# A graph-convolution kernel: a later turn for ScalarE's copies, rows fetched for every 48th quad, gates as tanh

## The chip, the cores and the metric

The kernel runs on one core of one Trainium2 chip. The core has five engines, each with a queue of its own that it works off in order: TensorE (PE in the profile, with its weight loads shown apart as PEld), VectorE (DVE), ScalarE (ACT), GpSimd (POOL) and SyncE (SP). SyncE and GpSimd start DMAs, and 16 DMA engines carry them out. The metric is the device time of one execution in microseconds (us); less is better.

## The reference

One equivariant graph convolution on 12,500 nodes and 400,000 edges (sorted by destination), with a residual and a layer norm behind it. Cut to what matters:

```python
h_s = s @ lin1_ws * a * _inv(S_IN)                       # per node, 64 numbers
h_v = jnp.einsum('nci,cd->ndi', v, lin1_wv) * ...        # per node, 32 x 3 numbers
hid = jax.nn.silu(edge_scalars @ fc_w1 * _inv(R))        # per edge
w = hid @ fc_w2 * _inv(FC_HID)                           # per edge, 224 weights
es, ev = h_s[edge_src], h_v[edge_src]                    # gather of 160 numbers per edge
# five products of w, es, ev and edge_attr: mid_s (96), mid_v (128 x 3)
agg_s = jax.ops.segment_sum(mid_s, edge_dst, n)          # sum at each destination
agg_v = jax.ops.segment_sum(mid_v, edge_dst, n)
pre_s = s @ sc_ws * a + agg_s @ lin2_ws * a              # scaled
pre_v = ...                                              # the same for the vectors
scalars = jax.nn.silu(pre_s[:, :64])
gated = jax.nn.sigmoid(pre_s[:, 64:96])[:, :, None] * pre_v
out = _layernorm(x + concat(scalars, gated))
```

All of it is float32. Silu of a number is the number times its sigmoid, so `scalars` is gated too.

## The kernel before

First the node table `h_tab` (12,500 rows of 160 numbers, 640 bytes each) is computed and written to memory; this is over after some 80 us. Then one long unrolled loop runs over 782 steps. A step works on a *quad*, four tiles of 128 edges. Six steps make a chunk, for which one pair of DMAs fetches the edges' 64 inputs (`es`, line 200, two buffers). The order on every engine is written out by hand: each engine does its instructions in the order in which the Python loop (line 869) issues them.

In step n, in the order of issue:

- `fetch(n + 4)` (line 724) loads the chunk that begins four steps later and the indices (SyncE).
- `fetch_rows(n)` (line 735): some quads, listed in `own` (line 461), are not gathered by GpSimd. SyncE fetches their 512 rows one by one, each with a register move and a DMA of 640 bytes (line 485), in 32 jobs of 16 rows; a job begins with a load of 16 addresses into registers (line 480). `OWN` is the distance of two such quads, and a job goes out on every `EVERY`th step. The rows go into one buffer `hq`, so the jobs of the next such quad begin when VectorE is through with the last one: they hang on `at_bytes` being multiplied on VectorE in step m - OWN + 2 (line 741).
- `gather` (line 452): for every other quad GpSimd issues four indirect DMAs, one for each tile (line 456), into `hg`, which has four buffers. So GpSimd can be four quads ahead of VectorE and no more.
- `weights` (line 490): four matmul halves give the 224 weights of each edge, in `pw` in PSUM (two buffers, line 498).
- In steps in which a node tile is finished, `turn(k)` (line 627) turns the sums of 128 nodes with two transposes on TensorE; VectorE scales them into `z` (line 637). The remaining parts, `gates` (Sigmoid on ScalarE), `gated`, `residual`, `moments`, `root` (Sqrt on ScalarE) and `norm`, follow one to a step for four node tiles at a time.
- VectorE: `one_hot` (line 561), which is its first to need the step's `pw`; four products of `pw` and `hg` into `pr` (lines 508 and 516); `select_quad` (line 570) into `sel`; then sums of finished blocks into `acc` (line 609).
- `sum_up` (line 824) of the quad of two steps ago: TensorE multiplies `sel` and `pr` into `pa` (line 577). When a pair of blocks is complete, `close` copies it to `sa` on ScalarE (line 790).
- `hide(n + 2)` (line 748), for every second quad: a matmul into `misc` (line 447) and silu on ScalarE into `hid` (line 449).
- `output` and `turn_blocks`: transposes of `sa` into `misc` (line 586), copies to `tt` on ScalarE (lines 589 and 591), and after 16 blocks the second linear map (line 601) with a copy `os` on ScalarE (line 604).
- `products_due`: the self-connection, 50 matmuls into `misc` (line 770), added by VectorE (line 771).

`misc` is two PSUM tiles used in turn by `hide`, `turned`, `second`, `turn` and the self-connection (class `Banks`, line 424). Before TensorE writes one again, the engine that read it last must be through.

Of the kernel before, what the change touches and what calls it, by code (L numbers as in the profile page):

```python
# [37 lines left out]
NF = 4  # L38
OWN = 68
BATCH = 16  # L40
EVERY = 2

# [15 lines left out]
def gnn_kernel(  # L58
# [127 lines left out]
    def in_pairs(a):  # L186

        return a.rearrange("o (c k h) -> o h c k", k=KB, h=2)

    ess = {}  # L190

    def load_chunk(c, queue=nc.sync):
        if c in ess:
            return
        t0, halves = chunks[c]
        es = ess[c] = loads.tile([2 * S, SIDE * P], F32, name="es")
        for half, n in enumerate(halves):
            to = es[half * S:(half + 1) * S]
            e0 = (t0 + half * halves[0]) * P
            queue.dma_start(to[:, :n * P], es_t[:, e0:e0 + n * P])  # L200

# [156 lines left out]


    load_chunk(0, nc.gpsimd)  # L360
    nc.gpsimd.dma_start(dt, dst)
    iota = consts.tile([P, W], F32, name="iota")
    nc.vector.tensor_copy(iota, iota_i)
# [73 lines left out]

    def hidden(pool, psum, es, halves, t0, n):

        ph = psum.tile([2 * S, Q * P], F32, name="ph", tag="misc")  # L440
        hid = pool.tile([2 * S, Q * P], F32, name="hid")
        ends = [max(0, min(n, m - t0)) for m in halves]
        assert ends[0] >= ends[1]
        for k, c0, c1 in ((2 * S, 0, ends[1]), (S, ends[1], ends[0])):
            if c1 > c0:
                c = slice(c0 * P, c1 * P)
                nc.tensor.matmul(ph[:k, c], w1[:k, :k], es[:k, t0 * P + c0 * P:t0 * P + c1 * P],  # L447
                                 start=True, stop=True)
                nc.scalar.activation(hid[:k, c], ph[:k, c], AF.Silu, scale=1.0 / math.sqrt(64))  # L449
        return hid  # L450
# [39 lines left out]
    def weights(psum, hid, slots):  # L490

        pw = psum.tile([P, Q, 256], F32, name="pw")
        n = len(slots)
        for t in range(0, n, 2):
            half, c = slots[t]
            m = min(2, n - t)
            assert half == 0 and all(slots[t + k] == (k, c) for k in range(m))
            nc.tensor.matmul(pw[:, t:t + m, :NWT], hid[:m * S, c * P:(c + 1) * P], w2[:m * S, :m],  # L498
                             start=True, stop=True)
        return pw  # L500

# [73 lines left out]
    def add_tile(pa, half, sel, t, pr, start, stop):  # L575

        nc.tensor.matmul(pa[half * ROWS:(half + 1) * ROWS, :NPR],  # L577
                         sel[:, t].rearrange("p k w -> p (k w)"), pr, start=start, stop=stop)

    def turned(psum, sa, tt, b, n):  # L580

        pt = psum.tile([P, 512], F32, name="pt", tag="misc")
        k = n * ROWS
        for four in range(4):
# [3 lines left out]

        nc.scalar.copy(tt[:, :6, b:b + n].rearrange("c (f k) b n -> c f k b n", f=2),  # L589
                       by[:, :2, 1:, :n])  # L590
        nc.scalar.copy(tt[:, 6:, b:b + n], by[:, 2:, 0, :n])  # L591

# [19 lines left out]
    def finish(fin, psum, t0, nt, p, most=NF):  # L612


        whole = nt if p == P else nt - 1
        spans = [(0, nt)] if t0 + nt == tiles_of_nodes else [(k, k + 1) for k in range(nt)]
        xt = fin.tile([P, most, D], F32, name="xt", bufs=2)
# [9 lines left out]
        def turn(k):  # L627
            if not held:
                held.extend(fin.tile([P, most, *shape], F32, name=name) for name, shape in (
                    ("z", [2 * V3]), ("sg", [V3]), ("y", [D]), ("st", [6]), ("mv", [2]),  # L630
                    ("rs", [])))
            z = held[0]
            c = (t0 + k) * P
            pp = psum.tile([P, 2, V3], F32, name="pp", tag="misc")
            for m in range(2):
                nc.tensor.transpose(pp[:, m], acc[:, m, c:c + P], ident[:V3, :V3])  # L636
            return lambda: nc.vector.tensor_scalar(
                z[:, k], pp.rearrange("p m c -> p (m c)"), at[:, t0 + k:t0 + k + 1], None,
                op0=OP.mult)

        def gates():
            z, sg = held[:2]
            nc.scalar.activation(sg[:, :nt], z[:, :nt, :V3], AF.Sigmoid)

        def gated():
            z, sg, y = held[:3]
            for k, m in spans:
                nc.vector.tensor_mul(y[:, k:m, :S], z[:, k:m, :S], sg[:, k:m, :S])  # L648
                nc.vector.tensor_mul(  # L649
                    y[:, k:m, S:].rearrange("p t (c i) -> p t i c", i=3),  # L650
                    z[:, k:m, V3:].rearrange("p t (i c) -> p t i c", i=3),
                    sg[:, k:m, None, S:].to_broadcast([P, m - k, 3, V]))

        def residual():
            y = held[2]
            for k, m in spans:
                nc.vector.tensor_add(y[:, k:m], y[:, k:m], xt[:, k:m])  # L657

        def moments():
            _, _, y, st, mv, _ = held  # L660
            for k in range(nt):
                nc.vector.bn_stats(st[:, k], y[:, k])  # L662
            for k in range(nt):
                nc.vector.bn_aggr(mv[:, k], st[:, k])  # L664

        def root():
            mv, rs = held[4:]
            nc.scalar.activation(rs[:, :nt], mv[:, :nt, 1], AF.Sqrt, bias=eps)  # L668

        def norm():  # L670
            _, _, y, _, mv, rs = held
            nc.vector.reciprocal(rs[:, :nt], rs[:, :nt])  # L672
# [5 lines left out]

        return [lambda k=k: turn(k) for k in range(nt)] + [
            gates, gated, residual, moments, root, norm]  # L680


# [6 lines left out]
    with tc.tile_pool(  # L689
# [34 lines left out]
        def fetch(n):  # L724

            if n < len(steps):
                c, i, tiles = steps[n]
                if i == 0:
                    load_chunk(c)
                for t, _, _ in tiles:  # L730
                    ahead(t)
# [3 lines left out]
        def fetch_rows(n):  # L735

            for m in own:
                if n == max(1, m - OWN - 6):
                    at_of[m] = places(mine, m)
                if n == m - OWN + 2:  # L740
                    nc.vector.tensor_scalar_mul(at_of[m], at_of[m], float(row_bytes))
                    hq_of[m], jobs = rows_of(mine, at_of[m])
                    rows_due.extend((m, job) for job in jobs)
            if n % EVERY == 0 and rows_due:
                rows_due.pop(0)[1]()
            assert all(m > n for m, _ in rows_due)

        def hide(n):
# [4 lines left out]
            if i % 2:  # L753
                return
            load_chunk(c)
            hids[c, i // 2] = hidden(edge, misc_ps, ess[c], chunks[c][1], 2 * i, 4)

        CHN = 500

        def self_connection(c0):  # L760
# [13 lines left out]
            return [lambda: part(0, scs, xs), lambda: part(1, scv, xv)]  # L774

        pas = {}
        tts = {}
# [10 lines left out]
        def close(j, n):  # L788
            sa = late.tile([P, NPR], F32, name="sa")
            nc.scalar.copy(sa, pas.pop(j)[:, :NPR])  # L790
            turns_due.append((n + 2, j, sa))

        def turn_blocks(n, j, sa):
            if not turns:
                tts[0] = late.tile([P, 8, NO, W], F32, name="tt", bufs=1)
            turned(misc_ps, sa, tts[0], len(turns), 2)
            turns.extend((2 * j, 2 * j + 1))
# [51 lines left out]
        to_do = list(jobs)  # L849
        turning, doing = [], []  # L850

# [10 lines left out]
        with tc.manual_schedule(engines={ENG.PE, ENG.DVE, ENG.Activation, ENG.Pool, ENG.SP}):  # L862
            fetch(0)
            hide(0)
            waits = []
            pieces = list(range(0, N, CHN))
            products_due = []
            checks = farthest(late)
            for n, (c, i, tiles) in enumerate(steps):
                if 2 <= n < 2 + ZP // 2:  # L870
                    for k in range(2):
                        clear(2 * (n - 2) + k)
                if n in checks:
                    checks[n]()
                fetch(n + 4)
                fetch_rows(n)
                hg = hq_of.pop(n) if n in own else gather(deep, [index(t) for t, _, _ in tiles])
                pw = weights(pw_ps, hids[c, i // 2], [(half, u - i // 2 * 4) for _, half, u in tiles])

                rest = turning.pop(0)() if turning else None  # L880
                step_on = not rest and doing.pop(0) if doing and not turning and not rest else None
                ready = []

                def first(n=n):
                    if rest:
                        rest()
                    ready.extend(add_up(n))
# [10 lines left out]
                if len(waits) > 2:  # L898
                    sum_up(n, *waits.pop(0))
                hide(n + 2)  # L900
                for blocks, in due(maps_due, n):
                    output(n, blocks)
                for j, sa in due(turns_due, n):
                    turn_blocks(n, j, sa)
                if products_due:
                    products_due.pop(0)()()
                if n % 30 == 13 and pieces:
                    products_due.extend([lambda: (lambda: None)] * 3 + self_connection(pieces.pop(0)))
            assert not pieces and not products_due
            last_steps = finish(fin, misc_ps, *last_job, most=LAST)  # L910
            n = len(steps)
            while waits:
                sum_up(n, *waits.pop(0))
            while turns_due or maps_due:
                n += 1
                for blocks, in due(maps_due, n):
                    output(n, blocks)
                for j, sa in due(turns_due, n):
                    turn_blocks(n, j, sa)
            assert len(adds) <= NO  # L920
            n += 2
# [19 lines left out]
        with tc.For_i(0, n_redo, 1):  # L941
# [9 lines left out]
            with tc.For_i(0, n_again, 1) as g, tc.For_i(0, GT, 1) as k:  # L951
# [21 lines left out]
                hg = gather(deep, [idx])  # L973
                pr = products(edge, weights(pw_ps, hid, [(0, 0)]), hg, 1)
                r = edge.tile([P, 1], F32, name="r", bufs=1)
# [74 lines left out]
```

## Time and profile before

| | |
|---|---|
| median of 6 runs | 5317.15 us (5298.61 to 5345.06) |
| the profiled execution | 5316.27 us, its span 5314.3 us |
| TensorE matmuls | busy 4001.6 us (75%) |
| GpSimd | busy 2947.3 us (55%) |
| VectorE | busy 2449.1 us (46%) |
| ScalarE | busy 921.8 us (17%) |
| mean granted TensorE clock | 0.864 of full speed |
| DMA | 412.51 MB, 78 GB/s |
| first gather, first and last row DMA of SyncE | at 61.2 us, 138.6 us and 5112.6 us |
| a step, from one `one_hot` to the next | 6.65 us in the mean |

A span runs from the program's first to its last instruction in the trace. Busy time of an engine counts its instructions alone, and not its waiting; DMA-issuing instructions of SyncE are not counted. Idle time in front of an instruction is put down to the semaphore update that ended it; "remote" means that the update is in the trace, but not which instruction made it. No engine is busy for the whole span, so the time is set by who waits for whom.

### The profile page before, as it was taken

The page shows a single profiled execution, that of the slowest core. Times are in us where ns is not written, and L with a number is a line of the kernel's source. Part 1 is how long each engine was busy: PE and PEld are TensorE (multiplying, and loading weights), DVE is VectorE, ACT ScalarE, POOL GpSimd, SP SyncE. Part 2 cuts the span into 40 slices and gives each one's busy share as a digit, 9 for nine tenths or more (in the row PEclk, how much of TensorE's full clock was granted, in tenths as well). Part 3 has the DMA queues.
Part 4 walks back from the last instruction along what each step waited for, and adds up shares of the span by engine and source line. Part 5 has one row for each costly group of instructions (what it writes and reads, how often), then busy time and mean ns, then how long its engine had stood idle before and what let it go on. Part 6 is the DMA issues. An engine that isn't in the chain of part 4 may idle for free. (4 is left out here: it accounts for less than half of the span.)

```text
span 5314.3 us, 58310 instructions
## 1 busy us (share of the span) xinstructions
PE 4001.6 (75%) x14291; PEld 1722.4 (32%) x14291; DVE 2449.1 (46%) x6607; ACT 921.8 (17%) x2463; POOL 2947.3 (55%) x3100
## 2 busy tenths in 40 slices
PE   6777767777777777777777777777777877777876
PEld 3333323333333333333233333333333333332333
DVE  4444443444444544444444445444444544444544
ACT  2111111111111111111111111111111111111212
POOL 4555555555555555555555555555555555555553
PEclk8888888888898888888888888888888888888888
DMA  6223222232323322332333332232232333223331
GB/s 185 73 72 80 75 74 73 74 78 73 78 74 77 80 72 71 83 81 63 74 78 75 76 80 72 72 83 73 72 83 71 73 77 80 76 69 82 77 79 51
DMA packets 243271, 412.51 MB, mean 78 GB/s; under 512 B 83147, under 2 KB 173575, under 8 KB 242023
## 3 DMA queue, kind: packets, MB, share of 16 engines
q0 software_dynamic: 150160, 262.93, 18.8%
q1 hardware_dynamic: 92246, 145.66, 11.5%
q8 instruction: 115, 1.88, 0.1%
q14 instruction: 236, 1.93, 0.1%
q10 hardware_dynamic: 514, 0.10, 0.0%
HBM read 392.43 MB, written 16.00 MB: 77 GB/s over the span
## 5 line engine op out<-in xcount | busy, mean ns | idle before, releaser
L456 POOL DMA_INDIRECT hg<-h_tab,idx x3081 | 2933.0, 952 | 2274.6 <-DVE pr L516 1230.7
L498 PE MATMUL pw<-w,hid 128*128 128x448 f32 x3126 | 1527.2, 615 | 259.9 <-ACT hid L449 133.5
L577 PE MATMUL pa<-pr,sel 128*64 128x416 f32 x6250 | 1358.5, 554 | 69.8 <-ACT sa L790 35.5
L561 DVE TENSOR_TENSOR pw<-rel,iota 128x64 f32<-128x64 int16 x782 | 182.6, 233 | 2534.8 <-remote 1388.9
L516 DVE TENSOR_TENSOR pr<-pw,hg 128x384 f32<-128x384 f32 x2313 | 1137.7, 548 | 0.0
L498 PEld LDWEIGHTS pw<-w,hid 128*128 128x128 f32 x3126 | 616.7, 215 | 795.3 <-issue 565.8
L586 PE MATMUL misc<-ident,sa 128*128 128x128 f32 x2084 | 375.5, 309 | 548.7 <-ACT tt L591 240.7
L577 PEld LDWEIGHTS pa<-pr,sel 128*64 128x64 f32 x6250 | 400.7, 144 | 972.5 <-issue 920.2
L790 ACT COPY sa<-pa 128x416 f32<-128x416 f32 x521 | 266.7, 512 | 1810.7 <-remote 620.7
L447 PE MATMUL misc<-es,w 128*128 128x512 f32 (+1 forms) x784 | 459.2, 669 | 156.1 <-ACT tt L591 105.4
L586 PEld LDWEIGHTS misc<-ident,sa 128*128 128x128 f32 x2084 | 266.5, 155 | 885.5 <-issue 302.9
L508 DVE TENSOR_TENSOR pr<-pw,hg 128x512 f32<-128x512 f32 x771 | 532.7, 691 | 28.1 <-DVE pw L561 1.3
L601 PE MATMUL misc<-tt,l 128*96 128x256 f32 (+5 forms) x1496 | 394.5, 417 | 83.8 <-ACT tt L591 51.9
L449 ACT ACTIVATE hid<-misc 128x512 f32<-128x512 f32 x392 | 235.1, 600 | 917.4 <-remote 537.0
L589 ACT COPY tt<-misc 128x192 f32<-128x192 f32 x521 | 166.4, 319 | 1150.9 <-remote 811.0
L601 PEld LDWEIGHTS misc<-tt,l 128*96 128x96 f32 (+1 forms) x1496 | 253.6, 182 | 247.2 <-issue 108.5
L570 DVE TENSOR_TENSOR sel<-pw,eas 128x256 f32<-128x256 f32 x782 | 325.1, 416 | 0.0
L447 PEld LDWEIGHTS misc<-es,w 128*128 128x128 f32 x784 | 121.4, 195 | 425.7 <-issue 260.3
L609 DVE TENSOR_TENSOR acc<-acc,os 96x32 f32 x1042 | 204.2, 196 | 25.6 <-ACT os L604 6.9
L771 DVE TENSOR_TENSOR acc<-acc,misc 96x500 f32<-96x500 f32 x50 | 33.6, 671 | 183.0 <-remote 102.5
L591 ACT COPY tt<-misc 128x64 f32<-128x64 f32 x521 | 117.1, 225 | 0.0
L636 PE MATMUL misc<-ident,acc 96*128 96x96 f32 x196 | 37.7, 279 | 101.5 <-DVE acc L609 43.2
(87 smaller groups left out, 705.5 us busy)
## 6 DMA issues: line engine op xcount, KB each, us to landing
es<-in_es_t_dram SPq DMA_DIRECT2D x258, 384.0 KB
hq<-h_tab SPq DMA_DIRECT2D x5632, 0.6 KB
hg<-h_tab,idx POOLq DMA_INDIRECT x3081
h_tab<-ht POOLq DMA_DIRECT2D x6, 1280.0 KB
xt<-in_x_dram SPq DMA_DIRECT2D x23, 320.0 KB
out_dram<-y SPq DMA_DIRECT2D x23, 320.0 KB
xv<-in_xv_t_dram SPq DMA_DIRECT2D x25, 187.5 KB
xs<-in_xs_t_dram SPq DMA_DIRECT2D x25, 125.0 KB
```

What stands on the lines that cost most here:

```text
L447: nc.tensor.matmul(ph[:k, c], w1[:k, :k], es[:k, t0 * P + c0 * P:t0 * P + c1 * P], start=True, stop=True)
L449: nc.scalar.activation(hid[:k, c], ph[:k, c], AF.Silu, scale=1.0 / math.sqrt(64))
L456: nc.gpsimd.indirect_dma_start(out=hg[:, t, :], out_offset=None, in_=h_tab, in_offset=bass.IndirectOffsetOnAxis(ap=i, axis=0))
L498: nc.tensor.matmul(pw[:, t:t + m, :NWT], hid[:m * S, c * P:(c + 1) * P], w2[:m * S, :m], start=True, stop=True)
L508: nc.vector.tensor_mul(two, pw[:, :n, :2 * S].rearrange("p t (k c) -> p t k c", k=2), hg[:, :n, None, :S].to_broadcast([P, n, 2, S]))
L516: nc.vector.tensor_mul(pr[:, :n, first:first + V3].rearrange("p t (i c) -> p t i c", i=3), pw[:, :n, None, 2 * S + k * V:2 * S + (k + 1) * ...
L570: nc.vector.tensor_mul(sel[:, :n], oh[:, :, None, :].to_broadcast([P, n, 4, W]), by_slot(tiles[0][0])[:, u:u + n, :, None].to_broadcast([P ...
L577: nc.tensor.matmul(pa[half * ROWS:(half + 1) * ROWS, :NPR], sel[:, t].rearrange("p k w -> p (k w)"), pr, start=start, stop=stop)
L586: nc.tensor.transpose(pt[:, four * P:four * P + k], sa[:k, c:c + P], ident[:k, :k])
L601: nc.tensor.matmul(po[:, k, :nb], l2[r, terms[to, part, four]], a[:, :nb], start=(n == 0), stop=(n == len(of) - 1))
L609: nc.vector.tensor_add(window, window, os[:, :, b])
L790: nc.scalar.copy(sa, pas.pop(j)[:, :NPR])
```

## The change

It does four things.

**Rows.** `OWN` goes from 68 to 48 and `EVERY` from 2 to 4, with a job now on three steps of four (`if n % EVERY`). The `own` quads are 16 and no longer 11 (steps 56, 104, ... 776 in place of 76, 144, ... 756).

**ScalarE's turn.** Silu, the copies to `tt` and the copy to `sa` are no longer issued where their input is made. They are put on lists and issued together by `catch_up()` in the next step, straight behind that step's `weights`. The first of them is given a dependence on the last weights matmul (`behind`, `marks[0]`), and since TensorE works in order this covers the others. `hide` is called for step n + 3 and comes last. The loads of `es` get the same dependence, on the weights of the step before.

**Gates.** sigmoid(x) is taken as (1 + tanh(x/2))/2: Tanh on ScalarE reads the turned sums in PSUM with a scale of half the node's attribute, one call for each node tile; VectorE forms (tanh + 1) times the sums in the free part of the same PSUM tile, and a third instruction multiplies by half the attribute and adds x. `z`, `sg` and the separate residual are gone. The VectorE part runs in the next step (`gates`).

**Order of the PSUM tiles.** A node tile is turned, or a self-connection piece done, only in even steps (`free`), in which `hide` does nothing.

```diff
-OWN = 68
+OWN = 48
-EVERY = 2
+EVERY = 4
...
+    def behind(ins, mark):
+        if mark is not None:
+            tc.add_manual_dep(ins.ins, mark.ins.name, mybir.DependencyInfo(
+                mybir.DependencyClass.Sync, mybir.DependencyReason.DATA), reason="order")
...
-            queue.dma_start(to[:, :n * P], es_t[:, e0:e0 + n * P])
+            ins = queue.dma_start(to[:, :n * P], es_t[:, e0:e0 + n * P])
+            behind(ins, mark)
...
-                nc.scalar.activation(hid[:k, c], ph[:k, c], AF.Silu, scale=1.0 / math.sqrt(64))
+                def activate(k=k, c=c):
+                    return nc.scalar.activation(hid[:k, c], ph[:k, c], AF.Silu,
+                                                scale=1.0 / math.sqrt(64))
+                if later is None:
+                    activate()
+                else:
+                    later.append(activate)
...
-        nc.scalar.copy(tt[:, :6, b:b + n].rearrange("c (f k) b n -> c f k b n", f=2),
-                       by[:, :2, 1:, :n])
-        nc.scalar.copy(tt[:, 6:, b:b + n], by[:, 2:, 0, :n])
+        copies = [lambda: nc.scalar.copy(tt[:, :6, b:b + n].rearrange("c (f k) b n -> c f k b n", f=2),
+                                         by[:, :2, 1:, :n]),
+                  lambda: nc.scalar.copy(tt[:, 6:, b:b + n], by[:, 2:, 0, :n])]
...
+            later.extend(copies)
...
-            return lambda: nc.vector.tensor_scalar(
-                z[:, k], pp.rearrange("p m c -> p (m c)"), at[:, t0 + k:t0 + k + 1], None,
-                op0=OP.mult)
...
-            nc.scalar.activation(sg[:, :nt], z[:, :nt, :V3], AF.Sigmoid)
...
+            half = half_at[:, t0 + k:t0 + k + 1]
+            nc.scalar.activation(g[:, k], pp[:, :V3], AF.Tanh, scale=half)
+            pg = pp[:, 2 * V3:2 * V3 + D]
+            def gate():
+                nc.vector.scalar_tensor_tensor(pg[:, :S], g[:, k, :S], 1.0, pp[:, :S],
+                                               op0=OP.add, op1=OP.mult)
+                nc.vector.scalar_tensor_tensor(
+                    pg[:, S:].rearrange("p (c i) -> p i c", i=3),
+                    g[:, k, None, S:].to_broadcast([P, 3, V]), 1.0,
+                    pp[:, V3:2 * V3].rearrange("p (i c) -> p i c", i=3),
+                    op0=OP.add, op1=OP.mult)
+                nc.vector.scalar_tensor_tensor(y[:, k], pg, half, xt[:, k],
+                                               op0=OP.mult, op1=OP.add)
+            return gate
...
-            if n % EVERY == 0 and rows_due:
+            if n % EVERY and rows_due:
                 rows_due.pop(0)[1]()
...
-            load_chunk(c)
-            hids[c, i // 2] = hidden(edge, misc_ps, ess[c], chunks[c][1], 2 * i, 4)
+            load_chunk(c, mark=marks[0])
+            hids[c, i // 2] = hidden(edge, misc_ps, ess[c], chunks[c][1], 2 * i, 4, later)
...
+        later, closed = [], []
+        marks = [None]
+        def catch_up():
+            fs = later + closed
+            later.clear()
+            closed.clear()
+            for k, f in enumerate(fs):
+                ins = f()
+                if k == 0:
+                    behind(ins, marks[0])
...
-            nc.scalar.copy(sa, pas.pop(j)[:, :NPR])
+            pa = pas.pop(j)
+            closed.append(lambda: nc.scalar.copy(sa, pa[:, :NPR]))
...
-                pw = weights(pw_ps, hids[c, i // 2], [(half, u - i // 2 * 4) for _, half, u in tiles])
-                rest = turning.pop(0)() if turning else None
+                pw, marks[0] = weights(pw_ps, hids[c, i // 2], [(half, u - i // 2 * 4) for _, half, u in tiles])
+                catch_up()
+                free = n % 2 == 0 or n + 3 >= len(steps)
...
                 if len(waits) > 2:
                     sum_up(n, *waits.pop(0))
-                hide(n + 2)
+                if free and turning:
+                    gates.append(turning.pop(0)())
+                elif free and products_due:
+                    products_due.pop(0)()()
                 for blocks, in due(maps_due, n):
                     output(n, blocks)
                 for j, sa in due(turns_due, n):
                     turn_blocks(n, j, sa)
-                if products_due:
-                    products_due.pop(0)()()
+                hide(n + 3)
```

## The prediction

> **What bounds the kernel now.** I began with the page's groups. GpSimd's gathers have the longest total:
>
> ```profile
> L456 POOL DMA_INDIRECT hg<-h_tab,idx x3081 | 2933.0, 952 | 2274.6 <-DVE pr L516 1230.7
> L498 PE MATMUL pw<-w,hid 128*128 128x448 f32 x3126 | 1527.2, 615 | 259.9 <-ACT hid L449 133.5
> L516 DVE TENSOR_TENSOR pr<-pw,hg 128x384 f32<-128x384 f32 x2313 | 1137.7, 548 | 0.0
> ```
>
> 3081 gathers take 952 ns each, and the timeline has 0.30 us between two of an unbroken series, so a quad costs 4 x 1.25 = 5.0 us. 771 quads make some 3770 us. The rest of GpSimd's time is idling until VectorE frees an `hg` buffer. In the trace I cut the gathers into series wherever GpSimd idles over 1 us: 304 series, 303 pauses, 1417 us, 4.68 us each. 61 us of start + 3770 + 1417 + 66 of tail and small gaps = 5314, the span; the median of 5317 is the same within 0.1%.
>
> So why is VectorE late? The view of waits:
>
> ```profile
> DVE pw L561 <- remote: 1388.9, 163, 16.2
> POOL hg L456 <- DVE pr L516: 1230.7, 268, 14.5
> ACT tt L589 <- remote: 811.0, 75, 17.4
> ACT hid L449 <- remote: 537.0, 70, 17.2
> PE misc L586 <- ACT tt L591: 240.7, 29, 10.4
> ```
>
> VectorE waits at `one_hot`, whose one wait is for TensorE's weights. Timeline of TensorE and VectorE in one such wait:
>
> ```profile
> 2522.23 1.67 PE L498 MATMUL pw<-w,hid 128*128 128x448 f32 x4
> ...
> 2531.82 0.23 DVE L561 TENSOR_TENSOR pw<-rel,iota 128x64 f32<-128x64 int16 x1 [8.84 <-remote]
> ```
>
> The weights were done at 2523.9 and VectorE began at 2531.82. The signal from TensorE was 7.9 us late, while gathers ran (to 2529.4); ScalarE's wait for the transposes ended at 2530.40, as late. In the clean case the same step takes 0.04 us. I compared each `one_hot` with the end of its weights: 227 waits of more than 2 us, 1539 us together, and 180 of them end in a pause of GpSimd, in the median 2.5 us after its last gather. The cycle is: gathers run; signals of TensorE get stuck; buffers run out; GpSimd stops; the signals come through; VectorE frees a buffer 2.4 us later.
>
> SyncE suffers in the same stretches. Its timeline in a pause and in a series:
>
> ```profile
> 2511.98 3.78 SPq L485 DMA_DIRECT2D hq<-h_tab  x12
> ```
>
> ```profile
> 2520.28 10.01 SPq L485 DMA_DIRECT2D hq<-h_tab  x10
> ```
>
> 0.32 us for a row in the first, 1.00 in the second. I sorted all distances from row to row by whether gathers were moving data (from 3.5 us after a series begins to 1.7 us after its last one, where SyncE's instructions turn slow and fast again). Without those over 4 us, which are waits: 2234 rows in 2675 us, 1.20 us each, while gathers moved; 3310 rows in 1486 us, 0.45 us, otherwise. The long ones are 814 us. The sum is 4975, the stretch from the first row to the last.
>
> **The change, part by part.**
>
> *Rows.* 5 more quads go to SyncE. GpSimd is spared 20 gathers, 25 us, and with 2.53 quads to a series two pauses, 9 us: -34 us. SyncE gets 5 x 512 = 2560 rows more, each a move and a DMA, 160 register loads and 20 small index loads: 8192 rows in place of 5632. At the mixed 0.75 us they would take 6144 us, more than the span. But SyncE's lateness makes pauses, and in pauses it is fast, so I solve for a balance. With T the span, 61 + 3061 x 0.952 + (3061 - N) x 0.30 + 4.68 N + 66 = T, for N pauses. Gathers move data for the length of the series less 1.8 us each. For N = 430 the series last 3703 us and data moves for 2930, some 2850 of it inside the stretch of rows. In that 2850 / 1.20 = 2381 rows are issued. The other 5811 take 2609 us at 0.45. The single buffer `hq` makes SyncE wait at each own quad for VectorE:
>
> ```profile
> SPq L480 <- DVE pw L561: 211.4, 9, 33.3
> SPq L480 <- DVE at_bytes L741: 53.6, 2, 40.0
> ```
>
> 265 us for 11, 24 each, 16 of them 384 us. A late SyncE waits less, since VectorE then stands at that quad; I take between none and all, 190. The stretch of rows is 2850 + 2609 + 190 = 5650. Ahead of it lie 130 us (first job in step 10) and behind it 100 (six steps and the tail): T = 5880, from 5690 to 6070 with the waits. N from T gives 437, so it closes. With the same rates the old schedule needs 2675 + 1486 + 265 + 340 = 4770 of 5314, which is why SyncE binds nothing today: no `one_hot` of an own quad waits for rows (gaps before its products 0.03 to 0.17 us). Bounds of the rates: 1.00 and 0.39 (0.32 plus a sixteenth of a 1.2 us register load) give 5310; 1.43 and 0.51, with all waits counted into the rows, give 6220.
>
> Where SyncE is late, two things stop: VectorE at an own quad, and `es`, which stands behind the rows in SyncE's queue. Today 17 us lie in the median between the issue of `es` and its matmul, under 6 in 11 of 128. `hide(n + 3)` takes one step (6.65) off that, and the new wait for the weights of the step before holds all later rows with it. This is the way in which a late SyncE throttles every chunk.
>
> *ScalarE's turn.* Of TensorE's signals, those of lines 447, 586 and most of 577 are no longer waited for; some 3.3 to a step become about 1.3. Signals come in order, so a stuck weights signal is no longer behind others. In 102 of the 227 waits another signal of TensorE came first, 3.67 us ahead of VectorE's: 374 us that VectorE could get at most. Against it, ScalarE starts its copies behind the next weights, and TensorE needs them for the next `misc`. Covered in clean steps: silu 0.60 and the copies 0.32 + 0.22 lie beside the 1.62 us of the sum-up. Where the signal is stuck the cover is gone and TensorE stands one `misc` group earlier (1.12 + 0.66 = 1.8 us) in up to 227 cycles: up to 400 us. Behind ScalarE's waiting instruction in its queue stand the copy `sa` and the sorted edge attributes (0.24 us each), for which VectorE's `sel` waits; that has 2.4 us of products as cover. So -374 to +400, and as the two ends are alike I take 0.
>
> *Gates.* VectorE loses 0.41 + 0.22 + 0.28 + 0.32 = 1.23 us for a node tile and gets three instructions between 0.82 (the old SBUF ones) and 1.37 us (the z, 128x384 and 128x256 ones): -40 to +14 us over 98 tiles on an engine 46% busy, taken as 0. ScalarE gets 98 Tanh between 0.23 and 0.51 us (its PSUM copies) for 25 Sigmoids of 0.5 us: +10 to +37 us. Its table loads:
>
> ```profile
> L449 ACT ACT_TABLE_LOAD x48 | 61.6, 1283 | 35.2 <-issue 32.5 <-PE misc L447 1.9
> ```
>
> Silu is loaded again after each Sigmoid and each Sqrt. If Tanh lies with silu, 98 loads become 50, -62 us; if not, 246, +190 us. ScalarE is 17% busy; cover gone, 98 x 2 x 1.28 = 251 us in front of copies that TensorE needs. I take 0, since between these the row of loads decides nothing.
>
> The Trainium skill ("ScalarE: Activation LUTs", "Table sets: the hidden batching unit") speaks against this part: it lists tanh in the set of sigmoid, and this trace shows that silu is loaded again after sigmoid. By that page Tanh would bring the 246 loads, and the sum would go up by the 190 us or less; by the rows of ScalarE's busy time it stays hidden.
>
> *PSUM order.* At most two `misc` tiles to a step; no instruction more or less. 0.
>
> Sum: 5880 from SyncE's balance, in which the 34 us are included. I say 5850, as the lateness of SyncE takes a little of the waits away.
>
> **Rivals.**
>
> *A, faster: the weights signal, now first in line, frees VectorE while gathers run, and SyncE's rows get cheaper with it.* For it: 102 waits in which another signal came first. Against it: nothing in the change alters the gathers, in whose stretches SyncE is slow. Half of the 374 us and the 34 give 5090; all, 4910; if the pauses were halved, 5314 - 34 - 709 = 4570. It decides if a row under gathers costs under 0.76 us (then 8192 fit into 5317; measured 1.20), and for 5090 it must cost 0.68.
>
> *B, slower by ScalarE's wait:* SyncE keeps pace, but TensorE stands for the stuck weights: 5314 - 34 + 400 = 5680, half of it 5480. For it: TensorE already waits 241 us for `tt` at line 586. Against it: the fewer signals.
>
> *C, no difference:* the gains in signals and SyncE's lateness cancel, 5320.
>
> **How the numbers follow.** SyncE's rows 0.48, with its own range 5310 to 6220; A 0.37, from 4570 to 5290; B 0.10; C 0.05. The range: of A I leave out what lies under 4980 (about 0.12), of the first what lies above 6230 (0.06): 4980 to 6230. A measurement of this kernel can tell a difference of about 0.5%, 27 us. Slower: 0.48 + 0.10 = 0.58; same 0.05; faster 0.37.
>
> **What would show it.** Right: SyncE's rows go on without a break from one own quad to the next, over 350 us for 512 rows; VectorE or GpSimd idle with `hq` as releaser, or TensorE at line 447 with `es`, by hundreds of us; more than 350 pauses of GpSimd. Wrong: rows during gathers at 0.7 us or less; fewer than 300 pauses; ScalarE and VectorE released at one instant and early. For the tables: 50 loads or about 246. What would make it wrong above all is that the slowness during gathers is not the gathers' own but depends on what TensorE signals.

## The result, and the profile after

The changed kernel takes 6063.5 us (median of 20 runs, 6041.8 to 6093.8) against 5325.3 us for the old one (46 runs, 5298.6 to 5379.2): the ratio is 1.138, with a 95% interval from 1.136 to 1.140. The forecast was 5850. The profiled execution has a span of 6055.7 us.

One thing has to be known for all that follows. These times and both traces are from one set of measurements; on which chip it ran is not on record. The experiments ran later on three chips, numbers 14, 4 and 0, on which the old kernel takes 3971 to 3973 us and not 5325, and the changed one 4343: a ratio of 1.093 there, from 1.091 to 1.095. I call them the first set and the later chips, and compare numbers across them only where that is said.

The groups of the changed kernel's profile (line 473 is the gather, 456 the `hide` matmul, 578 `one_hot`), from the page:

```profile
L473 POOL DMA_INDIRECT hg<-h_tab,idx x3061 | 2894.8, 946 | 3059.4 <-DVE pr L533 1701.7
...
L578 DVE TENSOR_TENSOR pw<-rel,iota 128x64 f32<-128x64 int16 x782 | 182.2, 233 | 3185.3 <-PE pw L515 1481.4
L456 PE MATMUL misc<-es,w 128*128 128x512 f32 (+1 forms) x784 | 530.9, 766 | 951.8 <-DMA es<-in_es_t_dram 759.6
```

The gathers cost what they did (946 ns for 952). GpSimd idles 3059 us in place of 2275. New is the last line: TensorE stands 760 us for `es` at the hidden layer's matmul, a wait that was not among the large ones before (26 us). The view of waits has further lines to look at:

```profile
DVE pw L578 <- PE pw L515: 1481.4, 397, 24.7
DVE pw L578 <- remote: 1376.1, 197, 13.3
...
POOL hg L473 <- DMA hq<-h_tab: 372.7, 32, 20.1
...
PE misc L785 <- DMA xs<-in_xs_t_dram: 228.3, 17, 18.8
```

VectorE waits for weights as before, but now mostly because TensorE makes them late, not because the signal is late. From the distances between the end of the weights and `one_hot`: late signals of over 2 us fell from 227 with 1539 us to 183 with 1135 us, while the idle time in which the weights themselves were not yet done rose from 897 to 1928 us. What TensorE itself waits for has changed places: of its idle time ahead of matmuls, 51 us were put down to DMAs before and 1010 now (`es` 760, the self-connection's input `xs` 228), while the part put down to ScalarE fell from 884 to 517 us.

The line with `hq` has to be read with care. GpSimd does not read `hq`; its gathers read the indices `idx`, which SyncE loads too, and these loads count on the same semaphores as the rows. In 30 of these 32 waits an `idx` load on a semaphore that the gather waits for was issued 4.5 to 7 us before the gather began. So most of this line (81 us in 12 waits before) is GpSimd waiting for its indices. VectorE, which does read `hq`, never waits for it: at all 16 own quads its first product starts within 0.17 us of its instruction before, 12 to 18 us after the last row was issued.

SyncE's timeline from one own quad to the next (start, length, instruction, count; line 502 is the row, 206 `es`):

```profile
1596.66 5.00 SPq L502 DMA_DIRECT2D hq<-h_tab  x10
1608.33 1.15 SPq L206 DMA_DIRECT2D es<-in_es_t_dram  x2
1627.09 35.84 SPq L502 DMA_DIRECT2D hq<-h_tab  x48
1663.03 1.11 SPq L206 DMA_DIRECT2D es<-in_es_t_dram  x2
1665.71 43.41 SPq L502 DMA_DIRECT2D hq<-h_tab  x80
1709.23 1.11 SPq L206 DMA_DIRECT2D es<-in_es_t_dram  x2
...
1956.75 14.35 SPq L502 DMA_DIRECT2D hq<-h_tab  x32
1979.73 1.15 SPq L206 DMA_DIRECT2D es<-in_es_t_dram  x2
```

Within an own quad the rows follow each other with nothing but SyncE's other loads between them, 512 in 342.0 us in the mean. Between the last row of one and the first of the next lie 23.9 us, in which SyncE mostly stands. 365.9 us is the cycle of 48 steps, 7.6 us a step; it was 6.65. How this reaches TensorE, later in the same cycle:

```profile
1897.43 11.54 SPq L502 DMA_DIRECT2D hq<-h_tab  x27
...
1909.06 1.12 SPq L206 DMA_DIRECT2D es<-in_es_t_dram  x2
...
1916.18 2.05 PE L456 MATMUL misc<-es,w 128*128 128x512 f32 x2 [14.49 <-DMA es<-in_es_t_dram]
```

`es` comes to its turn when the rows ahead of it are out, TensorE has been waiting since 1901.7, and the matmul starts when the transfer has landed, 6 us after its second half was issued.

### The profile page after: what moved, and what is told of

Same layout as the page of the kernel before. It is cut to its first block, busy times and chain, and to the rows that moved or that the text cites. A ratio compares the mean times of both kernels' runs of the same rounds, so it can differ in the third digit from the quotient of the medians.

```text
span 6055.7 us, 63034 instructions
## 1 busy us (share of the span) xinstructions
PE 4034.9 (67%) x14291; PEld 1737.2 (29%) x14291; DVE 2449.2 (40%) x6524; ACT 853.2 (14%) x2488; POOL 2909.0 (48%) x3080
## 5 line engine op out<-in xcount | busy, mean ns | idle before, releaser
L473 POOL DMA_INDIRECT hg<-h_tab,idx x3061 | 2894.8, 946 | 3059.4 <-DVE pr L533 1701.7
L594 PE MATMUL pa<-pr,sel 128*64 128x416 f32 x6250 | 1347.7, 551 | 231.2 <-ACT sa L819 221.9
L456 PE MATMUL misc<-es,w 128*128 128x512 f32 (+1 forms) x784 | 530.9, 766 | 951.8 <-DMA es<-in_es_t_dram 759.6
L515 PEld LDWEIGHTS pw<-w,hid 128*128 128x128 f32 x3126 | 667.6, 223 | 678.2 <-issue 643.0
L603 PEld LDWEIGHTS misc<-ident,sa 128*128 128x128 f32 x2084 | 253.7, 157 | 699.0 <-issue 376.6
L456 PEld LDWEIGHTS misc<-es,w 128*128 128x128 f32 x784 | 141.4, 226 | 1069.3 <-issue 974.1
L623 PE MATMUL misc<-tt,l 128*96 128x256 f32 (+5 forms) x1496 | 352.0, 383 | 4.4 <-ACT tt L608 3.7
L623 PEld LDWEIGHTS misc<-tt,l 128*96 128x96 f32 (+1 forms) x1496 | 225.6, 164 | 134.0 <-issue 56.2
L785 PE MATMUL misc<-xs,scs 64*96 64x500 f32 x50 | 41.3, 920 | 228.3 <-DMA xs<-in_xs_t_dram 228.3
```

The lines of the kernel that those rows point to most:

```text
L473: nc.gpsimd.indirect_dma_start(out=hg[:, t, :], out_offset=None, in_=h_tab, in_offset=bass.IndirectOffsetOnAxis(ap=i, axis=0))
L515: last = nc.tensor.matmul(pw[:, t:t + m, :NWT], hid[:m * S, c * P:(c + 1) * P], w2[:m * S, :m], start=True, stop=True)
L594: return nc.tensor.matmul(pa[half * ROWS:(half + 1) * ROWS, :NPR], sel[:, t].rearrange("p k w -> p (k w)"), pr, start=start, stop=stop)
L603: nc.tensor.transpose(pt[:, four * P:four * P + k], sa[:k, c:c + P], ident[:k, :k])
L623: nc.tensor.matmul(po[:, k, :nb], l2[r, terms[to, part, four]], a[:, :nb], start=(n == 0), stop=(n == len(of) - 1))
```

## The experiments

Twelve kernels ran, in four sets, each beside the old kernel: the first four on chip 14, the next four on chip 4, the last four on chip 0. The old kernel's medians there are within 0.1% of each other. I call *pace* the time of a step (from `one_hot` to `one_hot`) between the first and the last row of an own quad, and *job* the time of 16 rows with their load, as 1/32 of that stretch.

**Which part costs the time.** The changed kernel with the old row schedule (the first diff), and the old kernel with the new one (the second):

```diff
-OWN = 48
+OWN = 68
-EVERY = 4
+EVERY = 2
...
-            if n % EVERY and rows_due:
+            if n % EVERY == 0 and rows_due:
```

```diff
-OWN = 68
+OWN = 48
-EVERY = 2
+EVERY = 4
...
-            if n % EVERY == 0 and rows_due:
+            if n % EVERY and rows_due:
```

> The changed kernel with OWN 68 and a job on every second step again; ScalarE's turn, the gates, the PSUM order and the dependence of es stay. Theory 'rows' (SyncE's 8192 rows set the pace): SyncE has slack again, the es waits of TensorE at the hide matmul fall from 760 us to under 100, and the time is near the old one, 5200 to 5450 us. Theory 'turn' (ScalarE waiting for the next weights, and es with it, costs the time): 5700 us or more, with ScalarE's wait for the weights above 1500 us in front of the transposes' copies and TensorE waiting for tt. If both share it, between 5450 and 5700.

Measured: 3964.8 us, ratio 0.9986 (0.9976 to 0.9996). TensorE's waits for `es` are 24.9 us.

> The old kernel with OWN 48 and a job on three steps of four, nothing else. Theory 'rows': 5850 to 6100 us, rows without a break, some 365 us from own quad to own quad, es and hq as releasers with hundreds of us. Theory 'turn': 5300 to 5450 us, the rows fit in.

Measured: 4288.3 us, ratio 1.080 (1.078 to 1.082). The times in the expectations were made for the first set; the order they foretell is clear. The rows alone bring 8.0 of the 9.3% and without them the rest of the change is worth 0.14%. Here no late signal hides the pattern: the cycle is 257.7 us, 238.6 for the rows and 19.1 of standing, and SyncE's waits show for whom:

```profile
SPq L480 <- DVE pw L561: 230.1, 15, 19.1
```

15 waits of some 15 us are SyncE at the first load of the next own quad, until VectorE reaches that step.

**Without rows.** Both kernels with `own = []`.

> The changed kernel with an empty list of own quads: GpSimd gathers all 782 quads, SyncE only loads es, indices and node data. Theory 'rows': the pace is GpSimd's again; 3125 gathers at 1.25 us are 3910, some 307 pauses of 4.7 us 1440, and 127 of start and tail: about 5480, from 5250 to 5600. Theory 'turn': 5800 us or more even here. If SyncE's rows themselves are what makes TensorE's signals late (their traffic, not the gathers'), the pauses go: under 4900.

> The old kernel with an empty list of own quads. By the same sum about 5480 us. Set against the changed kernel without rows it gives the price of ScalarE's turn, the gates and the PSUM order by themselves: theory 'rows' says within 3% of each other; theory 'turn' says this one is 400 us or more the faster. If SyncE's rows are what makes signals late: under 4900 here too.

Measured: 4013.2 us for the changed kernel (ratio 1.0104, 1.0087 to 1.0121) and 4021.7 for the old one (1.0128, 1.0111 to 1.0145). The two agree within 0.2%, so ScalarE's turn, the gates and the PSUM order cost and bring next to nothing where the rows don't bind. The sum of 5480 missed, since its pauses are not there on this chip: without rows GpSimd makes at most one pause over 1 us, and 3125 gathers at 1.2535 us are 3917 of the 4011. Without rows the bound is GpSimd.

**The change itself on a later chip.**

> The changed kernel itself, beside the old one on the chip of this set. If the old kernel takes about 5320 us here: 6060. If it takes about 3970, as it did beside the first four kernels, where no signal of TensorE was late: theory 'rows' says one own quad to the next takes what the old kernel with these rows took there, 258 us (237 for 512 rows with their loads and 20 of waiting for VectorE), so 4250 to 4350 us, 7 to 10% slower than the old one; theory 'turn' says that ScalarE's turn adds to that, over 4450.

Measured: 4342.8 us, ratio 1.093 (1.091 to 1.095). The cycle is 261.4 us: 239.2 of rows and 22.2 of standing. As theory "rows" said, with 55 us more than the old kernel with these rows.

**Taking the standing away.** The changed kernel with two `hq` buffers and the jobs begun six steps earlier:

```diff
-        hq = pool.tile([P, Q, D], F32, name="hq", bufs=1)
+        hq = pool.tile([P, Q, D], F32, name="hq", bufs=2)
...
-                if n == max(1, m - OWN - 6):
+                if n == max(1, m - OWN - 12):
...
-                if n == m - OWN + 2:
+                if n == m - OWN - 4:
```

> The changed kernel with two hq buffers; the jobs of an own quad begin six steps earlier, so SyncE need not stand still until VectorE is through with the last own quad. Nothing else. Theory 'rows': the 20 to 24 us of waiting in each of 16 own quads go: with the old kernel at 3970 us, rows of one own quad need 237 us and 48 steps of GpSimd's pace need 243, so SyncE is no longer the bound and the time is 3930 to 4000 us; with the old kernel at 5320, 340 us of rows still stand against 319: 5650 to 5800. Theory 'turn' or es as such: no change from the changed kernel.

Measured: 4261.1 us, ratio 1.072. A miss: 82 us less than the changed kernel, where some 340 were expected. The standing is still 16.1 us of a cycle of 255.7. The 32 jobs still fill 43 of the 48 steps, three of four; in the 5 steps without a job SyncE is quickly through its list and waits for VectorE again, with two buffers as with one.

**Taking `es` out of SyncE's queue.** `load_chunk(c, queue=nc.scalar, ...)`.

> The changed kernel with es loaded from ScalarE's queue, one hq buffer as before. Theory 'rows, with es behind them as the way in which SyncE holds all others up': TensorE's wait for es goes, rows are waited for at the own quads alone, and a cycle is 512 rows (220 us without the es issues where the old kernel takes 3970, 340 where it takes 5320) and some 15 of waiting against 48 free steps (243 or 319): 3960 to 4080 us in the first case, 5650 to 5900 in the second. If the order of es is not the way: the time of the changed kernel, within 1%.

Measured: 5485.9 us, ratio 1.380. It doesn't answer its question, as the edit brought a wait of its own. The view of SyncE's waits:

```profile
SPq L502 <- DMA es<-in_es_t_dram: 1513.3, 193, 20.0
```

It was 150.3 us with 2.3 at most before the edit. In the trace a row's DMA waits for the semaphore that it will itself count up, and `es` loads count on the same few; in all 106 of SyncE's gaps over 5 us ahead of a row, an `es` load on the row's semaphore was issued by ScalarE only after SyncE had begun to wait (8.7 us after in the median), and the row went out 2.5 to 5.5 us behind that issue. While `es` is issued by SyncE it is ahead of the rows; issued by ScalarE at some later time, it holds the row that is next on its semaphore.

**Fewer own quads, the same density.** The changed kernel with `OWN = 56`: 13 own quads, still a job on three steps of four.

> The changed kernel with OWN 56 (13 or 14 own quads), all else as in it. Theory 'rows': a cycle of SyncE (258 us or 366) is to be set against 56 steps (284 at 5.07, 372 at 6.65): where the old kernel takes 3970, SyncE fits and GpSimd is spared 10 gathers against the old one: 3940 to 3980 us; where it takes 5320, it is on the edge: 5250 to 5500. Theory 'turn': no better than halfway between the changed kernel and the one with OWN 68.

Measured: 4263.8 us, ratio 1.074. A miss of theory "rows" as I had put it: 258 us of SyncE's work were to fit into 56 steps, 284 us. In the trace the rows take 235.2 us and then comes a gap of 64.4. So SyncE has time over in each cycle and the kernel is slow all the same. The pace in the stretch of rows is 5.58 us and outside it 4.62. A job takes 7.35 us; three in four steps are 5.5 us a step, more than GpSimd's 5.0. My reading is that what SyncE falls behind in 43 steps it can't have saved up before: its order is fixed, and it can be ahead only by what its own waits allow. This gave a new theory, "density", for the next two.

**Density against count.** `OWN = 56` with three jobs in five steps; and `OWN = 48` with the two buffers and the early start of above and two jobs in three steps:

```diff
-OWN = 48
+OWN = 56
...
-            if n % EVERY and rows_due:
+            if n % 5 in (0, 2, 4) and rows_due:
```

```diff
-            if n % EVERY and rows_due:
+            if n % 3 and rows_due:
```

> The changed kernel with OWN 56 and a job on three steps of five instead of three of four; 13 own quads as in the run before with OWN 56. With the old kernel at about 3970 us: theory 'density' (what binds is the share of steps that carry a job: 0.75 x 7.35 us for a job of 16 rows is 5.5 us of SyncE for a step, measured pace 5.58; GpSimd needs 5.0): 0.6 x 7.35 is 4.4, below GpSimd's 5.0, so TensorE's waits for es vanish and 3073 gathers at 1.2535 plus 94 make 3946; from 3930 to 3975. Theory 'count' (the number of rows, or of own quads with their waits, is what costs): 4150 to 4270 again. With the old kernel at 5320 a job takes 10.7 us or more, 6.4 for a step: 5250 to 5500 by density, 5600 or more by count.

> The changed kernel (OWN 48) with two hq buffers as in the run before with them, and the 32 jobs spread over all 48 steps, two steps of three. Theory 'density': 0.667 x 7.4 and 0.3 for es and indices make 5.2 us for a step against 5.5 in the dense stretch before, and the 16 us without rows in each cycle are used: a cycle of 245 to 252 us and 4030 to 4150 us in all with the old kernel at 3970 (4261 with two buffers alone). Theory 'count': unchanged, 4240 to 4270. With the old kernel at 5320: 5600 to 5800 by density, above 5900 by count.

Measured: 3985.2 us (ratio 1.0038, 1.0025 to 1.0052) and 4127.7 us (1.039, 1.037 to 1.041). The first is 10 us above the range that I gave, in which the waits for `es` were to vanish; 105 us of them are left. Still, 279 us are gone by nothing but spreading the same jobs. The second is in its range. Eight of the kernels in a row (the waits for `es` are TensorE's at the `hide` matmul):

| kernel | own quads | jobs in a step | time, us | pace, us | waits for es, us |
|---|---|---|---|---|---|
| changed, rows of before | 11 | 0.50 | 3964.8 | 4.94 | 24.9 |
| changed, OWN 56, thin | 13 | 0.60 | 3985.2 | 4.98 | 104.9 |
| changed, two hq, even | 16 | 0.67 | 4127.7 | 5.13 | 221.9 |
| changed, OWN 56, es early | 13 | 0.75 | 4238.0 | 5.51 | 15.7 |
| changed, two hq | 16 | 0.75 | 4261.1 | 5.42 | 296.8 |
| changed, OWN 56 | 13 | 0.75 | 4263.8 | 5.58 | 287.3 |
| old, rows of changed | 16 | 0.75 | 4288.3 | 5.51 | 496.5 |
| changed | 16 | 0.75 | 4342.8 | 5.63 | 334.1 |

13 own quads at two densities differ by 279 us. 13 and 16 at the same density, with one buffer each, differ by 79. So the number of own quads counts too, and about in proportion: above the old kernel's time stand 292 us for 13 and 371 for 16, 22.5 and 23.2 for each. The density sets what each own quad costs (23 us at 0.75, 10 at 0.67 with two buffers, 1 at 0.60), the number how often it is paid. The pace at 0.75 is near 0.75 x 7.35 to 7.48 = 5.5 to 5.6 us. That product by itself proves nothing, as 32 jobs at this density span 43 steps whatever sets the time; it tells of a bound only where SyncE has work all through the stretch. It has at 0.75: gaps of over 1 us between SyncE's instructions inside the own quads are 3 to 4% of the time there, against 5% at 0.67, 10% at 0.60 and 22% at 0.50. At 0.60 and 0.50 the same 1/32 is 8.2 and 9.7 us, with SyncE's waits in it.

**Is `es` the way?** `OWN = 56` at three in four, and `es` issued four steps earlier:

```diff
+                if n + 8 < len(steps) and steps[n + 8][1] == 0:
+                    load_chunk(steps[n + 8][0], mark=marks[0])
                 fetch(n + 4)
```

> The changed kernel with OWN 56 and three jobs in four steps, and es issued four steps earlier in SyncE's order, so that some 20 us more lie between its turn and its first use; nothing else. Over 43 steps SyncE falls behind by 43 x (5.5 - 5.05) = 19 us. Theory 'es is the way in which SyncE holds the others': this slack takes up most of it, the 13 steps without jobs give it back: 3950 to 4080 us with the old kernel at 3970 (4264 without the earlier es). Theory 'the rows themselves, through hq, or the index loads': 4200 to 4270. With the old kernel at 5320: 5300 to 5600 by the first, 5700 or more by the second.

Measured: 4238.0 us, ratio 1.067; 26 us less than without the edit. A miss for the theory that `es` is the way: the time lies in the range of the other one, of the rows, `hq` or the index loads. TensorE's large waits for `es` are gone, and others are larger or new, in the view of waits:

```profile
PE misc L785 <- DMA xs<-in_xs_t_dram: 239.1, 17, 26.3
DVE acc L786 <- PE misc L785: 220.5, 17, 19.0
...
DVE y L669 <- DMA xt<-in_x_dram: 112.8, 14, 15.3
...
POOL hg L473 <- DMA idx<-in_src_dram: 98.9, 18, 12.5
```

Without the edit TensorE waited 91 us for `xs` and VectorE 8 us for `xt`. These are loads of the self-connection, the residual and the gathers' indices, which SyncE issues between the rows. So `es` is where the lateness shows first, and not the only way: the other loads that SyncE issues between the rows are late as well.

**The added dependence of `es`.** The changed kernel with `load_chunk(c)` in place of `load_chunk(c, mark=marks[0])`.

> The changed kernel without the added dependence of the es loads on the weights of the step before; everything else as in it. Beside an old kernel at 3970 us the changed kernel takes 4343 and the old one with the same rows 4288; from the last row of one own quad to the first of the next SyncE needs 22.2 us in the first and 19.1 in the second, and 16 times the difference is 50 us. Theory 'mark': es waiting for the weights in that gap, with the next rows behind it, is the difference: 4280 to 4305. Theory 'turn': the later silu, copies and hide are the difference: 4330 to 4350, unchanged.

Measured: 4342.4 us, ratio 1.093, unchanged, against the first theory. SyncE's waits with the dependence:

```profile
SPq L206 <- PE pw L515: 171.3, 24, 26.9
...
SPq L497 <- DVE at_bytes L756: 144.9, 16, 10.8
```

and without it:

```profile
SPq L497 <- DVE at_bytes L756: 303.1, 16, 36.5
```

Between two own quads `es` goes out some 9 us earlier (0.3 us behind the last row and not 9.2), and the next load of row addresses still starts 20.4 us behind that row: it waits that much longer for VectorE. The 55 us between the changed kernel and the old one with the same rows come with the later silu, copies and `hide`, with the gates or with the PSUM order; I did not take them apart.

## Why the prediction was right

**SyncE's rows as the bound: right.** Of the signs it named, 760 us of TensorE at the `hide` matmul with `es` as releaser are there, and 355 pauses of GpSimd (over 350; I had 430 of 4.68 us, they last 6.24). The sign of the rows came out only in part: 512 take 342 us and not over 350, and from quad to quad there is a break of 23.9. The experiments on the later chips show the cause by itself: the rows alone 8.0%, all without them 0.14%. In the first set the parts were not run apart; there it rests on the traces, in which TensorE's waits for DMAs grew by 959 us.

**Where SyncE is late, two things stop: half right.** VectorE at an own quad was the first of the two, and it never stops there. `es` was the second, and it is joined by `xs` and by the gathers' indices, which the prediction did not name.

**Its sum: 5880 for 6056, from two errors of different sign.** Rows while gathers move data cost 1.04 us (2712 of them) and not 1.20, otherwise 0.435 (5408) for 0.45: 5179 us for the 5459 predicted, 280 less. But all distances over 4 us are 658 us, where I had 190 for waiting: 468 more. The sum of both is the 188 by which the stretch of rows, 5837 us, exceeds my 5650. That 5880 came out within 3% is therefore in part luck, and the step from it down to 5850 went the wrong way.

Two terms make up the 468. One is SyncE's waiting from quad to quad, 359 us for 190. "A late SyncE waits less" holds only a little: 23.9 us lie between the last row of one own quad and the first of the next, 28.3 in the old kernel, since in the 5 steps without a job SyncE catches up and VectorE's turn then decides. The other term the sum didn't have at all: 56 long distances inside the own quads, 300 us. The prediction called all distances over 4 us waits, but of these 300 us SyncE is idle for 29. The rest is its own work, in 54 of the 56 with an `es` pair, often with indices and other loads and the next addresses behind it. The old trace could have told: 538 of its 814 us lie inside the own quads, and SyncE is idle in 233 of them.

**The balance over the whole span: right here, and wrong as a method.** I set the sum of rows against the span. On the later chips what decides is the time of a job times the share of steps that carry one, against the pace of the others. In the first set that product is 0.75 x 10.69 = 8.0 us (pace 7.98) against 6.65 before; the density was not varied there. Sum and density agree as long as jobs fill 43 of 48 steps. With `OWN = 56` the sum would have called it free, and it cost 7.4% on a later chip. The same error is in rival A's point of decision: a row under 0.76 us was to make 8192 of them fit. On a later chip a row costs 0.437 us while gathers move, 8192 are 3580 of 3971 us, and the kernel was slower by 9.3%.

**`es`:** its median distance from issue to use fell from 17 to 6.1 us, with 59 of 128 under 6 us (11 before). The prediction also feared the new dependence; it has no price that shows: taken away, the time stayed.

**ScalarE's turn at 0: right on the later chips**, within 0.2% where rows don't bind, at most 1.3% where they do. In the first set late signals to VectorE did fall by 404 us, close to the 374 that I gave as the most it could get, while the weights themselves were late by a thousand more. Whether that fall is the turn's or only the slower pace's was not tried.

**Gates at 0: right in each part.** VectorE's instructions for a node tile cost 0.22 + 0.26 + 0.38 = 0.87 us for the 1.23 before, some 36 us less over 98, or 28 by their busy time (I had -40 to +14). Tanh takes 33.4 us for the 13.0 of Sigmoid. The table loads, from the groups of ScalarE:

```profile
L683 ACT ACT_TABLE_LOAD x25 | 32.1, 1283 | 0.4
L460 ACT ACT_TABLE_LOAD x24 | 30.8, 1283 | 32.1 <-DMA dt<-in_dst_dram 31.7
...
L658 ACT ACT_TABLE_LOAD x1 | 1.3, 1283 | 0.0
```

50 and not 246: after each Sqrt one load, at silu or once at Tanh, serves them both until the next Sqrt. The Trainium skill ("ScalarE: Activation LUTs", "Table sets: the hidden batching unit") lists tanh in sigmoid's set, but in the set of exp as well, and does not say where silu lies. So the 246 loads did not follow from it, as the prediction had it: the trace of before shows silu loaded again behind sigmoid, and this trace shows silu and tanh served by one load.

**Rivals.** A fell by its own test in the first set (1.04 us a row, 355 pauses). B's place, ScalarE's wait for late weights, shows in long waits of ScalarE in front of `tt` (2060 us), but TensorE's waits for ScalarE fell, from 884 to 517 us. On a later chip such waits stand in the changed kernel with the rows of before too (1771 us), at no cost.

No version beat the old kernel by more than the 0.5% that can be told from no change; the changed kernel with the old rows is 0.14% faster.

## What to carry to other kernels

Work that is spread over steps on a queue with a fixed order has to fit step by step: set the time of one job times the share of steps that carry it against the pace of the rest, and not the sum against the span. Where it doesn't fit, the loads behind it in that queue come late, and moving the one that shows it first lets the next ones show it. A second buffer helped these bunched jobs little (82 of 371 us); spreading them over all steps brought 133 more.

Distances in a queue are waits only if the queue is idle in them: look at what was issued before calling them slack. And a wait that the profile puts down to a transfer the engine doesn't read is likely another transfer on the same semaphore.

## What the runs showed of the hardware

**One kernel, 5325 us in one set and 3971 to 3973 on three chips later.** What I had read from the first trace as the effect of gathers moving data, late signals of TensorE and slow instructions of SyncE, is not theirs alone. On the later chips the gathers take the same 946 ns; in the changed kernel with the rows of before there is one pause of over 1 us. In the changed kernel there no `one_hot` starts over 0.04 us after its weights and VectorE are ready, against 183 of over 2 us in the first set, and a row under gathers costs 0.437 us, not 1.04. Slower transfers are not it: the packets of the gathers' queue take 106 ns in the mean in the first set and 118 on the later chip. Whether it is the chip or something else of that set these runs don't show; no experiment ran there.

**A wait handed on by a shared semaphore.** With `es` on another queue, rows stood 1513 us for transfers whose data they don't need, as their DMAs count on the same semaphores; in each of the 106 long ones the transfer had not even been issued when the wait began.

**In these runs the mean granted clock is lower where TensorE is less busy.** On the later chips it is 0.972 at 91% busy, 0.935 at 86% and 0.839 at 68% (the kernel with `es` on ScalarE's queue); in the first set 0.864 at 75% and 0.824 at 67%. The matmuls show little of it: the weights' matmul took 557, 578 and 577 ns in the first three of these. In the first set it took 615 and 619, and why it is slower there these runs don't show.
